# Down's integer weights made one chunk every second round, in a generator of their own

## The chip, the cores and the metric

The kernel runs on one core of a Trainium2 chip. The metric is device time in microseconds; the kernel before was run three times: 442.52, 441.52 and 440.69 us, median 441.52.

## The reference, cut to what matters

```python
x = x + xattn(layernorm(x), ctx, ctx, ...)           # 32 x 64 rows of 512, 8 heads
x = x + ffn(layernorm(x), gate_w, gate_z, gate_s, up_w, up_z, up_s, down_w, down_z, down_s)

def ffn(x, ...):                                     # H = 512, I = 1792, groups of 128
    gate_proj = (gate_w - repeat(gate_z, 128)) * repeat(gate_s, 128)     # 512 x 1792
    up_proj   = (up_w   - repeat(up_z, 128))   * repeat(up_s, 128)       # 512 x 1792
    down_proj = (down_w - repeat(down_z, 128)) * repeat(down_s, 128)     # 1792 x 512
    return (silu(x @ gate_proj) * (x @ up_proj)) @ down_proj
```

The weights are integers of 0 to 15 with a zero point and a scale for every group of 128 rows and each column. All outputs are float32.

## The kernel before, in words

The 32 sequences are taken in pairs (16 pairs of 128 rows), and four pairs make a block of 512 columns, so there are four blocks (t = 0 to 3). The hidden width of 1792 is cut into 14 columns f of 128 (`FC`), the model width of 512 into four groups g (`KT`) and four output parts l (`LC`).

Weights are kept as integers: once, in block 0, the zero point is subtracted from each loaded integer, in place, in the tiles `ng`, `nu` (gate, up) and `nd` (down). The scales are applied later, to the products. Gate and up are subtracted by POOL (L310), in chunks of one group g by 256 or 512 columns, against zeros `z16` that a DMA has spread over the partitions. Down is subtracted by DVE (L301), one chunk of 128 x 512 for each f, against zeros `z8`. `wide` lists the column ranges: 256 columns first (f0, f1), then three times 512 (f2 to f5, f6 to f9, f10 to f13). The tile of `z8` and that of `z16` in the loop have one buffer each: the load of the next range must wait until the last subtraction has read the one before.

After a first stage, whose order is written out by hand (`START`), a loop of rounds runs, 28 rounds (`ROUNDS`) for a block. In a round each of two lanes does one group g of `gate_up` (L627): two pairs of matmuls into `pg` and `pu`, each with a high and a low part of the activations, and ACT multiplies each sum by a quotient of scales before the next group is added (L646). After four groups ACT makes `g` with the silu (L649), DVE makes `h` (L652), and POOL splits it into `hh` and `hl` (L662, L663). Six rounds (`LAG`) behind, `down` (L668) does two output parts l of a column f in a round: a pair of matmuls into `pd` (L681, L684), which DVE adds to `y` (L694). `pd` has two banks, `pg` and `pu` share four. Between these run the steps of attention for the next block (`ROUND_STEPS`), with tiles named for the pairs, as `pv_6to7`, `pe_6to7`, and `q_e_set`, which POOL divides by the softmax sums (L506).

In every round of block 0 the loop calls the generator `weight_steps` (L294), which yields after each subtraction, of gate and up as of down, in one line:

```python
if r < ROUNDS:
    advance(weights, 2 if r < 4 else 1 + r % 2)      # L930, L931
```

The generator goes range by range: eight chunks of gate and up, then down's chunks of that range in a row. Counted out, f0 and f1 come in rounds 4 and 5, f2 in round 5, f3 in 6, f4 and f5 in 7, f6 in 13, f7 in 14, f8 and f9 in 15, f10 in 21, f11 in 22, f12 and f13 in 23. The column f is used by `down` from round 6 + 2f on. The weights of the last two ranges are loaded in rounds 5 and 13 (`load_weights`, L275), issued by POOL; zeros, rows and contexts are loaded by SP, each in its queue's order.

The written order is the input of a scheduler, which sets each engine's final order of instructions; `tc.issue_after` keeps the steps of the inner `with` behind the newest named instructions. [...]

Of the kernel before, what the change touches and what calls it, by code (L numbers as in the profile page):

```python
# [9 lines left out]
F32 = mybir.dt.float32  # L10
# [5 lines left out]
ALU = mybir.AluOpType  # L16
# [10 lines left out]
def kernel(  # L27
# [41 lines left out]
    nc = tc.nc  # L69
    B, D, L = x.shape  # L70
    I = gate_w.shape[1]
    P = 128
    NH, HD = 8, L // 8
    KT = L // P
    FC = I // P
# [38 lines left out]
    with ExitStack() as fast:  # L114
# [53 lines left out]
        wide = [(0, FIRST)] + [(c, CW) for c in range(FIRST, I, CW)]  # L168
# [91 lines left out]
        nd = const.tile([P, FC, L], F32R, tag="nd", name="nd")  # L260
# [6 lines left out]
        def load_wide(w: bass.AP, src: bass.AP, at: int, n: int):  # L267

            newest["POOL"] = nc.gpsimd.dma_start(w[:, :, at : at + n], src[:, :, at : at + n]).ins

        def load_down(at: int, n: int):
            fs = slice(at // P, (at + n) // P)
            newest["POOL"] = nc.gpsimd.dma_start(nd[:, fs, :], down_rows[:, fs, :]).ins

        def load_weights(at: int, n: int):  # L275

            load_wide(ng, gate_rows, at, n)
            load_wide(nu, up_rows, at, n)
            load_down(at, n)

        def load_zeros(at: int, n: int, pool=zeros):

            z16 = pool.tile([P, 2, KT, n], BF16, tag="z16", name=f"z16_{at}")
            for m in range(2):
                nc.sync.dma_start(z16[:, m], z_rows[m, :, at : at + n].partition_broadcast(P))
            return z16

        def load_down_zeros(at: int, n: int):
            z8 = zeros.tile([P, KT, CW], U8, tag="z8", name=f"z8_{at}")[:, : n // P, :]
            zd = z8_dram[at // P * L : (at + n) // P * L]  # L290
            nc.sync.dma_start(z8.rearrange("p f l -> p (f l)"), zd.partition_broadcast(P))
            return z8

        def weight_steps():  # L294

            def of_down(at: int, n: int, z8: bass.AP):
                for i in range(n // P):
                    piece = nd[:, at // P + i, :]  # L300
                    nc.vector.tensor_tensor(piece, piece.bitcast(F32), z8[:, i, :], ALU.subtract)  # L301
                    yield

            late = iter(())
            for at, n in wide:
                z16 = early_zeros.pop(0) if early_zeros else load_zeros(at, n)
                pieces = [(m, g) for g in range(KT) for m in range(2)]
                for m, g in pieces if at else sorted(pieces):
                    piece = (ng, nu)[m][:, g, at : at + n]
                    nc.gpsimd.tensor_tensor(  # L310
                        piece, piece.bitcast(F32), z16[:, m, g, :], ALU.subtract
                    )
                    yield
                yield from late
                late = of_down(at, n, load_down_zeros(at, n))
                if at:
                    yield from late

        def top_steps():

# [377 lines left out]
        def finish(t: int):  # L698

            for a in range(0, PB, SET):  # L700
                p = t * PB + a
                r = rows.tile([P, SET, L], F32, tag="r", name=f"r_{p}")
                nc.sync.dma_start(r, x1_dram[:, p : p + SET, :])
                yield
                py = two_banks(f"py_{p}")
                with in_one_piece() as first_taken:
                    for i in range(SET):
                        for l in range(LC):
                            nc.tensor.transpose(
                                py[:, i, ts(l, P)], y_sb[t, l][:, ts(a + i, P)], ident  # L710
                            )
                            first_taken()
                nc.vector.tensor_tensor(r, py, r, ALU.add)
                nc.sync.dma_start(o_rows[:, p : p + SET, :], r)
                yield
# [23 lines left out]
        def check_bounds():  # L739
            ok = const.tile([P, 3], F32, tag="ok", name="ok")  # L740
            s_abs = const.tile([P, 3 * NS], F32, tag="s_abs", name="s_abs")
            s_2d = s_all.rearrange("p m n -> p (m n)")
            nc.vector.tensor_scalar(s_abs, s_2d, -1.0, None, ALU.mult)
            nc.vector.tensor_tensor(s_abs, s_abs, s_2d, ALU.max)
            s_ok = const.tile([P, 3 * NS], BF16, tag="s_ok", name="s_ok")
            nc.vector.tensor_scalar(s_ok, s_abs, S_MIN, None, ALU.is_ge)
            nc.vector.tensor_scalar(s_abs, s_abs, S_MAX, None, ALU.is_le)
            nc.vector.tensor_tensor(s_ok, s_ok, s_abs, ALU.mult)
            nc.vector.memset(ok, 1.0)
            nc.vector.tensor_reduce(ok[:, 0:1], s_ok, AX.X, ALU.min)  # L750
            top = const.tile([P, 1], F32, tag="top", name="top")
            nc.vector.tensor_reduce(top, n_sum[0], AX.X, ALU.max)
            nc.vector.tensor_scalar(ok[:, 1:2], top, N_MAX**2, None, ALU.is_le)

            z_ok = const.tile([NS, 3, P], BF16, tag="z_ok", name="z_ok")
            nc.vector.tensor_tensor(z_ok[:, 0:2, :], z_nat[:, 0:2, :], z_16, ALU.is_equal)
            nc.vector.tensor_tensor(z_ok[:, 2, :], z_nat[:, 2, :], z_8, ALU.is_equal)
            nc.vector.tensor_reduce(
                ok[:NS, 2:3], z_ok.rearrange("p m n -> p (m n)"), AX.X, ALU.min
            )  # L760
            nc.vector.tensor_reduce(top, ok, AX.X, ALU.min)
            yield
            p_ok = two_banks("p_ok")[0:1, 0, 0:1]
            nc.tensor.matmul(p_ok, top, ones[:, 0:1], start=True, stop=True)
            nc.vector.tensor_scalar(flag, p_ok, float(P), None, ALU.not_equal)


        def advance(steps, n: int = 1):
            for _ in range(n):
                next(steps, None)  # L770
# [26 lines left out]
        with (  # L797
# [9 lines left out]
            for p in range(PB):  # L807
                j, i = divmod(p, SET)
# [7 lines left out]
            def first_banks(name: str):  # L816
                return ps0.tile([P, 2, CW], F32, tag="s", name=name)

            early_zeros, weights = [], weight_steps()

            @contextmanager
# [66 lines left out]
        def two_banks(name: str):  # L888
            return ps_at.tile([P, 2, CW], F32, tag="at", name=name)
# [15 lines left out]
        ROUNDS = 2 * FC  # L905
        LAG = 6
        done = object()
        bounds = check_bounds()
        BOUNDS_AT = 3 * ROUNDS + FC + LC
        LAST_OUT = (NBLK - 1) * ROUNDS + FINISH_AT[1] + 2  # L910
        with ExitStack():
            for r in range(NBLK * ROUNDS + LAG):
                t, k = divmod(r, ROUNDS)
                if k == 0:
                    attend = attention_steps(t + 1) if t + 1 < NBLK else iter(())
                if k == LAG and t > 0:
                    finishing = finish(t - 1)
                next(lanes[0], done)
                advance(attend)
                if r >= LAG:  # L920
                    advance(downs)
                if r >= 2:
                    next(lanes[1], done)

                with ExitStack() as behind:
                    for ins in newest.values():
                        behind.enter_context(tc.issue_after(ins))
                    if r in (5, 13):
                        load_weights(*wide[(5, 13).index(r) + 2])
                    if r < ROUNDS:  # L930
                        advance(weights, 2 if r < 4 else 1 + r % 2)  # L931
                    else:
                        advance(tops, 1 + (r % 4 == 3))
                    if k in FINISH_AT or k + 2 in FINISH_AT or r == LAST_OUT:
                        advance(finishing)
                if r >= LAG:
                    advance(downs)
                if r == ROUNDS:
                    with tc.issue_after(newest["DVE"]):
                        last_quotients()  # L940
                if r == NBLK * ROUNDS:

                    traced = list(nc.cur_bb.bb.instructions)
                    for engine in nc.engines:
                        last = next(i for i in reversed(traced) if i.engine == engine)
                        with tc.issue_after(last):
                            tc.mark_branch_hint_location("other", "LikelyTaken", [engine])
                if r in (BOUNDS_AT, BOUNDS_AT + 4):
                    with tc.issue_after(newest["DVE"]):
                        next(bounds, None)  # L950
# [119 lines left out]
```

## Time and profile before

| what | us |
|---|---|
| time of the profiled execution | 442.62 |
| its span | 440.7 |
| median of the three runs | 441.52 |
| PE busy in the span | 407.3 |
| DVE, ACT, POOL busy in the span | 330.3, 305.9, 280.4 |
| down's 14 subtractions on DVE, first to last start | 52.0 to 129.9 |
| one of them: least, median, most | 0.673, 0.682, 2.385 |
| gate's and up's subtractions of 512 columns on POOL, mean | 1.16 |
| PE busy in 43 to 135 us | 83.8 of 92 |
| PE busy in 150 to 250 us | 99.25 of 100 |

The span is from the first to the last instruction of one profiled execution; some 1.9 us of its time lie outside. Times in the trace count from the span's start. The loop of rounds of block 0 runs from about 40 to 135 us. A matmul of 512 columns starts 0.233 us after the one before it where PE doesn't wait.

### The profile page before, as it was taken

How to read it: one execution, taken by the hardware profiler on the slowest of the kernel's cores; microseconds unless marked ns; L12 is line 12 of the kernel's file. 1: busy time of each engine (PE TensorE's matmuls, PEld its weight loads, DVE VectorE, ACT ScalarE, POOL GpSimd, SP SyncE). 2: the span in 40 equal slices, each digit the busy share in tenths (PEclk: the TensorE clock that was granted, in tenths of full speed). 3: DMA queues.
4: the chain of work that ended last, by engine and by line, in shares of the span. 5: the costliest groups of instructions: out<-in, count | busy, mean ns of one | idle time of the engine just before them, and what ended most of it. 6: DMA issues, size and time to landing. Idle time of an engine off the chain costs nothing.

```text
span 440.7 us, 10359 instructions
## 1 busy us (share of the span) xinstructions
PE 407.3 (92%) x4191; PEld 313.1 (71%) x4191; DVE 330.3 (75%) x514; ACT 305.9 (69%) x469; POOL 280.4 (64%) x292
## 2 busy tenths in 40 slices
PE   4768987989889999999999999989999999999992
PEld 4655755757668776887778787767778888887871
DVE  5988486798779875895879885896869655768673
ACT  2344895555957679776888679656788787777760
POOL 4385858653954447575788668765787878874321
PEclk9999998999999999999999999999999999999998
DMA  6399659188011200311010102400010022200002
GB/s 214 82 276 367 206 150 280 49 243 260 2 49 48 91 9 0 125 70 51 0 50 1 51 6 92 144 1 1 1 50 1 1 60 85 95 1 0 1 4 100
DMA packets 20911, 36.54 MB, mean 83 GB/s; under 512 B 1832, under 2 KB 7416, under 8 KB 20856
## 3 DMA queue, kind: packets, MB, share of 16 engines
q1 hardware_dynamic: 14056, 24.20, 16.7%
q0 software_dynamic: 6192, 11.01, 8.7%
q8 instruction: 35, 0.57, 0.5%
q10 hardware_dynamic: 608, 0.59, 0.4%
q14 instruction: 20, 0.16, 0.1%
HBM read 27.37 MB, written 8.42 MB: 81 GB/s over the span
## 4 chain that ended last, share of the span: by engine, by line
PE 51%; POOL 18%; DVE 11%; issue 11%; ACT 5%; DMA 1%; SPq 0%; POOLq 0%; DVEq 0%; ACTq 0%
PE pu L636 14%; PE pg L636 14%; PE pd L681 7%; PE pd L684 6%; POOL hl L663 5%; POOL squares L333 3%; POOL squares L331 3%; DVE y L694 3%; POOL hh L662 3%; DVE xn_set L112 2%; POOL nu L310 1%; POOL q_e_set L506 1%; ACT pu L646 1%; DVE nd L301 1%; POOL ng L310 1%
## 5 line engine op out<-in xcount | busy, mean ns | idle before, releaser
L694 DVE SCALAR_TENSOR_TENSOR y<-pd,s_all,y 128x512 f32<-128x512 f32 x204 | 150.0, 743 | 43.8 <-PE pd L684 41.1
L646 ACT ACTIVATE pg<-pg,s_q 128x512 f32<-128x512 f32 x168 | 111.6, 666 | 69.0 <-PE pg L636 67.5
L646 ACT ACTIVATE pu<-pu,s_q 128x512 f32<-128x512 f32 x168 | 111.0, 662 | 9.0 <-PE pu L636 9.0
L662 POOL CAST hh<-h 128x512 fp32r<-128x512 f32 x55 | 35.0, 637 | 96.8 <-DVE h L652 95.2
L681 PE MATMUL pd<-hh,nd 128*128 128x512 f32 x224 | 92.7, 414 | 4.0 <-DVE y L694 3.3
L636 PE MATMUL pg<-hTh,ng 128*128 128x512 f32 x224 | 90.4, 403 | 3.1 <-DVE hTl L579 1.6
L636 PE MATMUL pu<-hTh,nu 128*128 128x512 f32 x224 | 91.2, 407 | 1.7 <-POOL nu L310 1.6
L684 PE MATMUL pd<-hl,nd 128*128 128x512 f32 x224 | 89.0, 398 | 0.2 <-DVE hl L660 0.2
L636 PE MATMUL pg<-hTl,ng 128*128 128x512 f32 x224 | 89.1, 398 | 0.0
L636 PE MATMUL pu<-hTl,nu 128*128 128x512 f32 x224 | 89.1, 398 | 0.0
L663 POOL TENSOR_TENSOR hl<-h,hh 128x512 fp32r<-128x512 f32 x55 | 72.1, 1312 | 4.3
L652 DVE SCALAR_TENSOR_TENSOR h<-pu,s_all,g 128x512 f32<-128x512 f32 x56 | 41.8, 746 | 30.2 <-ACT g L649 19.5
L681 PEld LDWEIGHTS pd<-hh,nd 128*128 128x128 f32 x224 | 42.0, 188 | 20.6 <-DVE y L694 7.0
L333 POOL TENSOR_TENSOR squares<-squares 128x512 f32<-128x512 f32 (+1 forms) x46 | 55.1, 1198 | 1.6
L636 PEld LDWEIGHTS pg<-hTh,ng 128*128 128x128 f32 x224 | 42.3, 189 | 17.2 <-ACT pg L646 2.8
L636 PEld LDWEIGHTS pu<-hTh,nu 128*128 128x128 f32 x224 | 42.3, 189 | 16.8 <-POOL nu L310 2.5
L636 PEld LDWEIGHTS pg<-hTl,ng 128*128 128x128 f32 x224 | 42.4, 189 | 9.4
L636 PEld LDWEIGHTS pu<-hTl,nu 128*128 128x128 f32 x224 | 42.4, 189 | 9.0
L649 ACT ACTIVATE g<-pg,s_all 128x512 f32<-128x512 f32 x56 | 38.9, 694 | 14.1 <-PE pg L636 12.5
L684 PEld LDWEIGHTS pd<-hl,nd 128*128 128x128 f32 x224 | 42.1, 188 | 8.4 <-DVE hl L660 0.5
L310 POOL TENSOR_TENSOR nu<-nu,z 128x512 fp32r<-128x512 f32 (+1 forms) x16 | 17.2, 1076 | 4.2 <-DMA nu<-in_L_ffn_up_w_dram 4.2
L310 POOL TENSOR_TENSOR ng<-ng,z 128x512 fp32r<-128x512 f32 (+1 forms) x16 | 17.0, 1069 | 2.1 <-DMA z<-z_dram 2.1
(293 smaller groups left out, 467.9 us busy)
## 6 DMA issues: line engine op xcount, KB each, us to landing
c_set<-in_ctx_dram SPq DMA_DIRECT2D x6, 512.0 KB
x<-in_x_dram SPq DMA_DIRECT2D x6, 512.0 KB
z<-z_dram SPq DMA_DIRECT2D x6, 512.0 KB
ng<-in_L_ffn_gate_w_dram POOLq DMA_DIRECT2D x3, 1024.0 KB, 5.8
nu<-in_L_ffn_up_w_dram POOLq DMA_DIRECT2D x3, 1024.0 KB, 7.7
x_dram<-x SPq DMA_DIRECT2D x6, 512.0 KB
r<-x_dram SPq DMA_DIRECT2D x6, 512.0 KB
out_dram<-r SPq DMA_DIRECT2D x6, 512.0 KB
```

Source lines behind the costliest of these rows:

```text
L310: nc.gpsimd.tensor_tensor(piece, piece.bitcast(F32), z16[:, m, g, :], ALU.subtract)
L331: nc.gpsimd.tensor_tensor(square[:, :n], piece, piece, ALU.mult)
L333: nc.gpsimd.tensor_tensor(total[:, :n], total[:, :n], square[:, :n], ALU.add)
L636: nc.tensor.matmul(acc, w[:, g, ts(f, P)], half[:, g, :], start=(g == 0 and half is hi), stop=(g == KT - 1 and half is lo), skip_group_che ...
L646: nc.scalar.activation(acc, acc, AF.Copy, scale=by)
L649: nc.scalar.activation(g_sb, acc, AF.Silu, scale=by)
L652: ins = nc.vector.scalar_tensor_tensor(h_sb, acc, by, g_sb, ALU.mult, ALU.mult)
L662: nc.gpsimd.tensor_copy(hh, h_sb)
L663: ins = nc.gpsimd.tensor_tensor(hl, h_sb, hh.bitcast(F32), ALU.subtract)
L681: nc.tensor.matmul(pd, w, h_hi[t, f], start=(t, f) != LAST, stop=False, skip_group_check=True)
L684: nc.tensor.matmul(pd, w, h_lo[t, f], start=False, stop=True, skip_group_check=True)
L694: ins = nc.vector.scalar_tensor_tensor(y, pd, by, y, ALU.mult, ALU.add)
```

## The change

Down's subtractions leave `weight_steps` and get a generator `down_steps`, called in rounds of a list `DOWN_AT`: f0 in round 4, f1 in round 5, and every later f in round 2f + 3, three rounds ahead of its use. Each range's `z8` load is issued by the step that makes the range's first chunk. Gate and up keep their rounds, now written as a table, `WEIGHTS_AT`: two in rounds 0 to 3, one or two in rounds 8 to 13 and 16 to 21. Rounds 8 to 13 hold nine calls, of which the ninth (round 13) went to f6 before; now it makes the first chunk of the last range (its `z16` load included), so that all chunks of gate and up in that range are one call earlier.

```diff
         def weight_steps():
-            def of_down(at: int, n: int, z8: bass.AP):
-                for i in range(n // P):
-                    piece = nd[:, at // P + i, :]
-                    nc.vector.tensor_tensor(piece, piece.bitcast(F32), z8[:, i, :], ALU.subtract)
-                    yield
-
-            late = iter(())
             for at, n in wide:
                 z16 = early_zeros.pop(0) if early_zeros else load_zeros(at, n)
                 pieces = [(m, g) for g in range(KT) for m in range(2)]
...
                     yield
-                yield from late
-                late = of_down(at, n, load_down_zeros(at, n))
-                if at:
-                    yield from late
+
+        def down_steps():
+
+            for at, n in wide:
+                z8 = load_down_zeros(at, n)
+                for i in range(n // P):
+                    piece = nd[:, at // P + i, :]
+                    nc.vector.tensor_tensor(piece, piece.bitcast(F32), z8[:, i, :], ALU.subtract)
+                    yield
...
+        WEIGHTS_AT = {r: 2 for r in range(4)}
+        WEIGHTS_AT |= {r: 1 + r % 2 for at in (8, 16) for r in range(at, at + 6)}
+        DOWN_AT = [4, 5] + [2 * f + 3 for f in range(2, FC)]
+        down_weights = down_steps()
...
                         load_weights(*wide[(5, 13).index(r) + 2])
+                    if r in DOWN_AT:
+                        advance(down_weights)
                     if r < ROUNDS:
-                        advance(weights, 2 if r < 4 else 1 + r % 2)
+                        advance(weights, WEIGHTS_AT.get(r, 0))
                     else:
                         advance(tops, 1 + (r % 4 == 3))
```

In the compiled order, on DVE the four chunks f2 to f5 no longer stand together between the y of l = 0 and of l = 1 of column f1: f2 stays there, f3 comes behind `h` of f3, f4 behind the third y of f2, f5 behind the third y of f3, and the later ones likewise, one for each f. On SP the `z8` load of the first range moves behind the context load at 45 us, that of f6 to f9 ahead of the next context load, and that of f10 to f13 behind the `z16` load of the last range. PE's and ACT's order changes by a few places in columns f1 to f10.

## The prediction

> **What bounds the kernel now.** I read the page's slices first (PE at 9 tenths in nearly all from slice 17 on), then tables by stretch, then PE's waits where it is not full.
>
> ```profile
> 135.00:150.00 15.00, 15.00 (x140) 11.65 (x138) 14.20 (x27) 10.93 (x17) 5.73 (x7) 1.00 0.11 36
> 150.00:250.00 100.00, 99.25 (x1047) 76.50 (x1039) 77.06 (x115) 77.31 (x117) 67.48 (x71) 1.00 0.13 44
> ```
>
> Columns: stretch, its length, busy us of PE, PEld, DVE, ACT, POOL, clock, DMA share, GB/s. From 126 us on PE is full, and nothing edited reaches beyond 135 us of before. A microsecond that PE gains in block 0 is therefore kept to the end, unless lost again inside block 0. What PE loses there, as waits between 62 and 130 us (total, times, longest):
>
> ```profile
> PE pd L681 <- DVE y L694: 2.5, 3, 2.0
> PE pu L636 <- POOL nu L310: 1.6, 2, 1.4
> PE pe_6to L515 <- POOL q_e_set L506: 1.1, 1, 1.1
> PE pv_6to L450 <- DVE k_eT_set L427: 1.1, 1, 1.1
> PE pg L636 <- ACT pg L646: 0.3, 1, 0.3
> ```
>
> The first is one place, with the edited instructions in front of it (timeline of DVE; then the stretches, columns as above):
>
> ```profile
> 63.93 0.75 DVE L694 SCALAR_TENSOR_TENSOR y<-pd,s_all,y 128x512 f32<-128x512 f32 x1 [0.34 <-PE pd L684]
> 64.60 4.91 DVE L301 TENSOR_TENSOR nd<-nd,z 128x512 fp32r<-128x512 f32 x4
> 69.51 1.40 DVE L694 SCALAR_TENSOR_TENSOR y<-pd,s_all,y 128x512 f32<-128x512 f32 x2
> ```
>
> ```profile
> 68.33:70.30 1.97, 0.00 (x1) 0.00 (x1) 1.97 (x5) 0.46 (x1) 0.66 (x2) 1.00 1.39 398
> 70.30:71.40 1.10, 1.10 (x5) 0.92 (x6) 1.10 (x2) 0.10 (x1) 1.10 (x2) 0.99 1.36 387
> 71.40:74.80 3.40, 3.40 (x10) 2.64 (x9) 1.01 (x3) 2.48 (x4) 3.32 (x5) 0.50 1.00 284
> ```
>
> I write pd_1_3 for column f = 1, part l = 3, pg_5 for f = 5. Four Down chunks (f2 to f5) stand between the y of l=0 and of l=1 of column f1. Only two pd banks exist, so pd_1_3 waits for y_1_1: PE stands 1.97 us. One microsecond after it resumes, the granted clock is 0.50 for 3.4 us.
>
> **The change part by part.**
>
> *Work.* The same 14 subtractions (0.68 us alone; beside a POOL instruction up to 2.38, the second of the four above), the same four z8 loads, the same 24 gate/up subtractions of the loop. No engine gets more; only order changes, so I compared each engine's compiled instruction order. On DVE, f3, f4, f5 go behind h_3, y_2_2, y_3_2, and so on singly. On POOL the nu0 subtraction of the last 512 columns moves ahead of hh_7, ng2 ahead of hh_8, ng3 ahead of the softmax division (L506). On SP the z8 loads move later.
>
> *A. Start of the loop: 0.* z8 of f0 and f1 (128 KB) is issued behind c_set, which SP issues at 45.13; before it went at 21. f0 waits for the nd weights anyway:
>
> ```profile
> DVE nd L301 <- DMA nd<-in_L_ffn_down_w_dram: 2.3, 1, 2.3
> ```
>
> It starts at 52.01. c_set's packets are through by about 51; 128 KB at 184 to 388 GB/s (the table's rates at 44 to 52 us) is 0.3 to 0.7 us more. Behind f0 on DVE queue mx, less and y_0_0, which has 0.64 us of idle before it; so 0 to 1 us, I take 0.
>
> *B. 64 to 76 us: +3.7.* After y_1_0 comes one chunk (0.98 us in the trace, beside POOL's DMA issues), then y_1_1 at 65.6 and not 69.51; pd_1_3 goes at 67.47 without a wait. Gained: the row step 67.93 to 70.30 less the usual 0.233 us, 2.14. The half clock: nine matmul steps from 71.33 to 74.98 take 3.65 us instead of 9 x 0.233 = 2.10, so 1.55 more. Check by walking: PE reaches pg_5's third matmul pair at 72.2 (it waits for ACT as before) instead of 75.89.
> [...] The row has 0.50 for one window's length, 71.4 to 74.8; in the 3.4 us ahead of it PE was busy 1.45. I take the row: a mostly idle window is enough. The stand of 1.44 us at 124 left the clock at 1.00, so the limit lies between about 1.5 and 2 us.
>
> *C. 76 to 91 us: -0.7.* POOL gains less than PE: its ng0 subtraction must await the ng load (issued 62.87, 5.8 us to land), so it is 1.2 us early, not 3.7. ng3 (behind the layer norm's power, whose input DVE has ready at 82.6) then ends at 84.5, while PE wants it at 83.8 for pg_6's last pair. Before, ng3 ended at 87.57 and PE came at 89.61. Left: 3.0.
>
> *D. 91 to 101 us: +2.0.* The chunks f7 to f9 no longer stand before k_eT: the 1.1 us wait at pv_6to falls to about 0.35 (the key bias follows at once on xn_set), and of the two y waits (0.26, 0.30, with about 0.3 of slow restarts) half remain; pu_7's third pair fits in ahead. By walking, the score matmuls start at 101.0 instead of 105.96 (for equal work). Left: 5.0.
>
> *E. 101 to 120 us.* Here POOL decides.
>
> ```profile
> 107.75 1.17 POOL L310 TENSOR_TENSOR ng<-ng,z 128x512 fp32r<-128x512 f32 x1 [2.13 <-DMA z<-z_dram]
> 118.35 1.90 POOL L506 TENSOR_TENSOR q_e_set<-q_e_set,sm_6to 128x1024 f32<-128x1024 f32 x1
> 120.21 1.68 POOL L310 TENSOR_TENSOR ng<-ng,z 128x512 fp32r<-128x512 f32 x1
> 123.78 1.60 POOL L310 TENSOR_TENSOR nu<-nu,z 128x512 fp32r<-128x512 f32 x1
> ```
>
> ng0 waits for the z16 of the last columns. It was issued at 99.1 behind c_set and the z8 of the last chunks, and none of the three moved a byte while the weights (software queue) ran:
>
> ```profile
> q0 software_dynamic: 1195, 2.38, 135.1%
> ```
>
> That row, of 95 to 101 us, is the only queue of its answer; the weights end near 102, z16 lands 5.7 us later. After: h_5 goes ahead of xn_set, so hl_5 and the weight issues behind it are 4.85 us earlier and the weights end at 97.15; z8 (256 KB, 0.7 us at 379 GB/s) now follows z16. Landing 97.15 + 5.7 - 0.7 = 102.15. From there POOL does, up to the end of the division, seven subtractions at 1.13 (ng0 to ng3; before it were six), hh and hl of f7 and f8 (3.9 together) and the division, 1.90: 102.15 + 7.9 + 3.9 + 1.9 = 115.85. PE's walk brings it to pe_6to at 114.0. It stands 2.1 us there, before 1.12, and starts at about 116.05 instead of 120.31. Left: 4.25.
> [...]
>
> *F. 120 to 126 us: +1.7.* The last nu subtraction ends at 117.7, PE asks at 119.6: the wait of 1.44 (1.7 with restart) goes. Left: 6.0.
>
> *G. Clock after E: -0.8.* A stand of 2.1 us is at the limit found in B; whether it fills most of a window depends on where windows fall. Half of 1.55.
>
> *SP.* z8 of f6 to f9 waits for f5 (about 85.9) and now stands in front of c_set, which waits for pv_6to (93.4) anyway: 0. z8 of f10 to f13 waits for f9 (116.4) with the store of x behind it, wanted by nobody soon: 0; f10 is used at about 121, and z8 of f2 needed under 3 us from 61.11.
>
> *Sum.* 6.0 - 0.8 = 5.2 us. The profiled execution has span 440.7 and time 442.62; 442.62 - 5.2 = 437.4 us. That execution is 1.1 us above the median of the runs, 441.52, perhaps because others missed the slow window; against the median the gain is 4.1 us, 0.9%. About 0.5%, 2.2 us, is what a measurement of this kernel can tell from no change.
>
> **Rivals.**
>
> [...]
>
> 2. *A wait in each round instead of one large one.* Each chunk now stands between two y of one column (f3, f4, f5 ...), and y frees one of two banks. The two cases in the trace cost 0.26 and 0.30 us, 0.3 to 0.4 with restart. If 10 chunks cost 0.35, 3.5 us go: 442.62 - 1.6 = 441.0, no difference to tell. Against it: PE has one or more gate/up pairs (0.47 us each) between most pd pairs.
>
> 3. *Slower: the z16 load is no earlier.* Place: POOL's ng0 of the last columns. If it lands at 107.7 still (c_set or the weights hold it), nu0 delays hh_7 and ng3 the division: q_e ends at 121.4 instead of 120.25. PE is 1.1 us late at pe_6to, gets 0.45 ahead by the vanished nu wait, but has stood over 5 us, so at least one slow window, 1.55: 443.7. It decides from a landing of about 107 on; at 106 it is a tie. For it: POOL is busy from 107.75 to 125 with hardly a gap, so lateness there passes straight to PE. Against: everything that releases the load comes 4 to 5 us earlier.
>
> 4. *f0 late.* If z8 of f0 lands after 53, each microsecond holds pd_0, mx and exp; at 3 us late, 440.5.
>
> **How the numbers follow.** Forecast 0.55 (435.4 to 439.3), rival 1 0.15, rivals 2 and 4 together 0.18, rival 3 0.12. Faster by over 0.5% (under 439.3): 0.70; within: 0.18; slower: 0.12. The range leaves out rival 3 and the far end of rival 1: 434.3 to 441.6.
>
> **What would show it.** No PE stand near 68 us and clock 1.00 up to 100 us (B); a wait of some 0.7 us of PE for POOL's ng, a new one (C); the pv_6to wait under 0.5 (D); ng0's DMA wait ending near 102 and PE's wait for q_e_set about 2 us, the largest left (E); no PE wait for nu after it (F). Wrong, if the slow window appears without a stand before it, if z16 lands after 105, or if pd's waits for y sum to over 2 us.

## The result, and the profile after

The changed kernel takes 443.08 us (median of 12 runs), the kernel before beside it 441.70 us (12 runs): a ratio of 1.0017, 95% interval 0.9999 to 1.0035. So there is no difference that can be told; the forecast was 437.4 us (435.4 to 439.3). The profiled execution took 443.27 us, its span is 441.5.

A stand is time in which PE waits. The stands of PE from 40 to 140 us in the changed kernel that bear on the forecast (us in total, times, longest; lines between them left out):

```profile
PE pe_6to L511 <- POOL q_e_set L502: 2.2, 1, 2.2
PE pd L677 <- DVE y L690: 2.0, 2, 1.4
...
PE pg L632 <- POOL ng L301: 0.9, 1, 0.9
PE pu L632 <- POOL nu L301: 0.7, 1, 0.7
```

The stand at pd_1_3 is down from 2.0 to 0.58 us, and the wait at pv_6to is gone, as forecast; so is the wait of 1.4 for nu near 124. What is new is a stand of 1.4 us at pd_5_1 near 97, behind a subtraction of Down (f6) that waits for its z8:

```profile
96.04 0.69 DVE L312 TENSOR_TENSOR nd<-nd,z 128x512 fp32r<-128x512 f32 x1 [1.16 <-DMA z<-z_dram]
97.45 0.50 PE L677 MATMUL pd<-hh,nd 128*128 128x512 f32 x1 [1.41 <-DVE y L690]
```

And the stand at pe_6to has doubled (the kernel before, then the changed one):

```profile
120.31 1.16 PE L515 MATMUL pe_6to<-w_T,q_e_set 64*64 64x64 f32 x64 [1.12 <-POOL q_e_set L506]
120.56 1.99 PE L511 MATMUL pe_6to<-w_T,q_e_set 64*64 64x64 f32 x64 [2.24 <-POOL q_e_set L502]
```

It costs more than its 2.24 us, as the table by stretch of the changed kernel shows (length, then busy us of PE, PEld, DVE, ACT, POOL; granted clock; DMA share; GB/s):

```profile
91.00:101.00 10.00, 8.45 (x164) 5.88 (x164) 8.12 (x12) 3.79 (x7) 1.86 (x3) 1.00 1.15 329
101.00:119.89 18.89, 16.40 (x126) 11.82 (x124) 15.15 (x21) 15.08 (x22) 14.38 (x13) 1.00 0.28 90
119.89:126.72 6.83, 6.16 (x74) 5.18 (x75) 2.34 (x3) 2.34 (x3) 4.01 (x4) 0.50 0.11 38
```

From 119.89 us, within the stand, the granted clock is 0.50 for 6.83 us. The same products start in the two traces as follows:

| product | before | after | ahead |
|---|---|---|---|
| pe_4to (softmax weights of pairs 4, 5) | 76.56 | 74.22 | 2.34 |
| pv_6to | 96.82 | 94.28 | 2.54 |
| pss_6to (scores) | 105.03 | 104.15 | 0.88 |
| pe_6to | 120.31 | 120.56 | -0.25 |
| po_6to | 126.10 | 127.39 | -1.29 |

(Around pss_6to a few gate and up products change places, so 0.88 is a lower end.) The changed kernel enters the loop 0.5 us late in this trace (its first pg at 39.48 instead of 38.99); 0.4 of it stands already at 15 us (a pq of the first stage, at 15.50 instead of 15.11), before anything edited runs. So what the first bundle of Down gains is 2.8 us. It is gained by 76 us, and all of it is lost between 95 and 127 us.

Why POOL is late for pe_6to stands in its timeline (start, duration, line, operation; in brackets what it waited for), here in the changed kernel; the prediction shows the same work before:

```profile
106.11 1.17 POOL L301 TENSOR_TENSOR ng<-ng,z 128x512 fp32r<-128x512 f32 x1 [4.09 <-DMA z<-z_dram]
107.54 1.17 POOL L301 TENSOR_TENSOR nu<-nu,z 128x512 fp32r<-128x512 f32 x1 [0.26 <-DMA z<-z_dram]
118.61 1.90 POOL L502 TENSOR_TENSOR q_e_set<-q_e_set,sm_6to 128x1024 f32<-128x1024 f32 x1
```

z16 of the last columns lands at 106.11, not at 102.15 as forecast (before: 107.75). The division ends at 120.51, 0.26 later than before. What fills the queues in front of z16, from the list of DMA issues (changed kernel; KB each, us from issue to landing); then SP's issues of z8 and of z16, and the whole traffic of 91 to 95 us:

```profile
ng<-in_L_ffn_gate_w_dram POOLq DMA_DIRECT2D x1, 1024.0 KB, 9.3
nu<-in_L_ffn_up_w_dram POOLq DMA_DIRECT2D x1, 1024.0 KB, 11.7
nd<-in_L_ffn_down_w_dram POOLq DMA_DIRECT2D x1, 1024.0 KB, 15.5
```

```profile
89.10 0.32 SPq L291 DMA_DIRECT2D z<-z_dram  x1
95.92 1.43 SPq L285 DMA_DIRECT2D z<-z_dram  x2
```

```profile
DMA packets 466, 0.93 MB, mean 231 GB/s; under 512 B 14, under 2 KB 14, under 8 KB 466
...
q0 software_dynamic: 333, 0.68, 63.0%
q1 hardware_dynamic: 133, 0.24, 36.4%
```

Before, these three took 5.8, 7.7 and 9.9 us. In the changed kernel SP issues the z8 of f6 to f9 (256 KB) at 89.10, in the middle of POOL's three weight issues (88.47, 89.30, 90.03). From 91 to 95 us the two queues together (q0 the weights, q1 what SP issues) move 231 GB/s, where the next six microseconds have 393. A slow start alone doesn't make this: before, the weights moved 42 GB/s in their first 2.2 us, but 397 from 95 us on. The last weights land near 105.5, and z16, issued at 95.92, comes behind them.

### The profile page after: what moved, and what is told of

Same layout as the page of the kernel before. It is cut to its first block, busy times and chain, and to the rows that moved or that the text cites. A ratio compares the mean times of both kernels' runs of the same rounds, so it can differ in the third digit from the quotient of the medians.

```text
span 441.5 us, 10362 instructions
## 1 busy us (share of the span) xinstructions
PE 409.5 (93%) x4191; PEld 315.7 (72%) x4191; DVE 332.5 (75%) x514; ACT 305.5 (69%) x469; POOL 281.6 (64%) x292
## 4 chain that ended last, share of the span: by engine, by line
PE 52%; POOL 16%; DVE 12%; issue 10%; ACT 5%; DMA 4%; SPq 0%; POOLq 0%; DVEq 0%; ACTq 0%
PE pu L632 14%; PE pg L632 14%; PE pd L677 8%; PE pd L680 7%; POOL hl L659 5%; POOL squares L329 3%; DMA z<-z_dram 3%; POOL squares L327 3%; POOL hh L658 2%; DVE y L690 2%; DVE xn_set L112 2%; POOL q_e_set L502 1%; DVE q_e_set L479 1%; DVE nd L312 1%; DMA x<-in_x_dram 1%
```

## Experiments

All times are medians beside the kernel before on the same chip, and the ratios are to its own medians: 442.23 us (the single edits, both together, f2 to f5 spread), 442.49 (the control, f6 to f13 spread, the group of ng, the filled stand), 442.63 (the last range's Down weights on the runs with early zeros, the tiny instruction) and 441.98 (the same weights as the changed kernel's one edit).

**Two single edits and both together.** POOL's order as before:

```diff
-        WEIGHTS_AT |= {r: 1 + r % 2 for at in (8, 16) for r in range(at, at + 6)}
+        WEIGHTS_AT |= {r: 1 + r % 2 for at in (8, 16) for r in range(at, at + 6)} | {13: 1}
```

> The changed kernel with POOL's order put back: the last range's subtractions begin in round 16 again, so one subtraction fewer (1.15 us) stands before hh of f7 and before the softmax division. Theory (the 256 KB of z8 beside the last weights is the cause): the zeros z16 still land at about 106, PE still stands 1.4 us for f6's chunk near 97; the division ends 1.15 us earlier (119.4), the stand at pe_6to falls from 2.2 to about 1.1, which is below what halves the clock, and a wait for nu of up to 1 us returns: 439.5 to 441.5. Rival (POOL's order alone is the cause): about 438, with the waits at 97 and for z16 harmless. Rival (neither matters, a small wait at each chunk eats the gain): 443, as the changed kernel.

441.08 us, ratio 0.9969 (0.9954 to 0.9984): 0.5% under the changed kernel.

Down's zeros early and small:

```diff
-            z8 = zeros.tile([P, KT, CW], U8, tag="z8", name=f"z8_{at}")[:, : n // P, :]
+            z8 = zeros.tile([P, 2, CW], U8, tag="z8", name=f"z8_{at}", bufs=3)
...
+        ZEROS_AT = {4: [0], 7: [1, 2], 11: [3, 4], 19: [5, 6]}     # round: pairs of columns
...
+                    for j in ZEROS_AT.get(r, []):
+                        z8_of[j] = load_down_zeros(2 * P * j, 2 * P)
```

> The changed kernel with Down's zeros loaded by pairs of columns in three small buffers, f6 to f9 in round 11 (about 77 us) and f10 to f13 behind the last z16, so that no z8 load runs beside the last weights (issued 88.5 to 90.8). Theory: the three weight loads land again 5.8, 7.7 and 9.9 us after issue instead of 9.3, 11.7 and 15.5; f6's chunk does not wait (1.16 us), PE's stand of 1.4 us near 97 goes; z16 lands near 103 instead of 106.1, the division ends near 117.5, PE's stand at pe_6to is under 1 us and the half clock of 6.8 us after it is gone: 437.5 to 439.5. Rival (the z16 load is held by the context load or by the weights, not by z8): z16 at 106, 441.5 to 443. Rival (small waits at each chunk): 442 to 443, waits for y unchanged.

439.57 us, ratio 0.9957 (0.9937 to 0.9977). The traffic of 91 to 95 us, with the weights issued at the same moment as in the changed kernel (88.51 for 88.47):

```profile
DMA packets 727, 1.46 MB, mean 364 GB/s; under 512 B 16, under 2 KB 16, under 8 KB 727
```

Both edits together, called the combined run below:

> Both edits together: Down's zeros early, and POOL's old order. Theory: as with the zeros alone, and the division 1.15 us earlier still, with a wait for nu behind it possible: 437 to 439. If the zeros alone make no difference but POOL's order does: as the run with POOL's order alone. If small waits at each chunk eat the gain: 442 to 443.

439.04 us, ratio 0.9930 (0.9905 to 0.9956). The traffic of 91 to 95 us in this run, and then its z16, its division and its pe_6to:

```profile
DMA packets 792, 1.60 MB, mean 401 GB/s; under 512 B 16, under 2 KB 16, under 8 KB 791
```

```profile
103.55 1.16 POOL L301 TENSOR_TENSOR ng<-ng,z 128x512 fp32r<-128x512 f32 x1 [3.32 <-DMA z<-z_dram]
114.60 1.90 POOL L500 TENSOR_TENSOR q_e_set<-q_e_set,sm_6to 128x1024 f32<-128x1024 f32 x1
```

```profile
116.55 1.16 PE L509 MATMUL pe_6to<-w_T,q_e_set 64*64 64x64 f32 x64 [0.97 <-POOL q_e_set L500]
```

With the 256 KB of z8 out of the way, 1.46 MB (zeros alone) and 1.60 MB (both, where the weights leave 0.55 us earlier) move in the four microseconds instead of 0.93; in the combined run the weights take 6.4, 9.1 and 11.9 us. The wait of f6's chunk for its z8 (1.16 us) and PE's stand behind it at pd_5_1 are gone in both runs with early zeros, and z16 comes 1.8 us (zeros alone) and 2.6 us (both) earlier. POOL's order is worth something of its own: with it put back, PE's stand at pe_6to is 1.1 us instead of 2.2, with the zeros where the change put them. The two gains are 0.5% and 0.6% apart and 0.9% together, each against the changed kernel; with some 0.2% of noise on each, whether they fully add can't be told. The early zeros missed their forecast in two points: z16 landed at 104.31 and not near 103, and the stand at pe_6to stayed at 2.24 us, since PE came earlier too; but no half clock followed it (see the last section).

**What the spreading itself is worth.** On the combined run: all of Down's chunks in bundles again (control), only f2 to f5 spread, only f6 to f13 spread.

```diff
-        DOWN_AT = [4, 5] + [2 * f + 3 for f in range(2, FC)]
+        DOWN_AT = [4, 5, 5, 6, 7, 7, 13, 14, 15, 15, 21, 22, 23, 23]        # control
+        DOWN_AT = [4, 5, 7, 9, 11, 13, 13, 14, 15, 15, 21, 22, 23, 23]      # f2 to f5 spread
+        DOWN_AT = [4, 5, 5, 6, 7, 7] + [2 * f + 3 for f in range(6, FC)]    # f6 to f13 spread
```

In the first and the third the zeros of f2 to f5 are loaded in round 5 and not 7.

> Control: the same early loads of Down's zeros by pairs and POOL's old order as in the combined run, but all of Down's chunks in their bundles, as in the kernel before. Theory: the zeros cost the kernel before nothing (its z8 never ran beside the weights), so this is the kernel before within 0.3%: 441 to 442.5, with the stand near 68 and the wait at pv_6to back. Rival (the gain of the combined run comes from the early zeros and not from spreading the chunks): 439 to 440.

> The last kernel, with f6 to f13 in their bundles again (rounds 13, 14, 15, 15 and 21, 22, 23, 23): only f2 to f5 are spread. Theory: the stand of 1.97 us near 68 and its half clock are gone (2.8 us, of which POOL's ng takes 0.7 at once), the wait of 1.1 us at pv_6to and the y waits near 97 stay: 439 to 440.5. Rival (what is gained at 68 is lost again wholly by 120, since POOL's division decides): 441.5, as the kernel before.

> The combined run with f2 to f5 in their bundle again (rounds 5, 6, 7, 7) and only f6 to f13 spread. Theory: PE stands about 2 us again near 68, with a half clock behind it in many executions, and z16 and the division come 2 to 3 us later; what the other columns gain (1.1 at pv_6to, 0.5 at y) stays in part: 440 to 441.5. If the two parts add, its gain over the control and the first bundle's gain over the control sum to the combined run's gain (3.2 us over the kernel before). If only the later columns matter: 439, as the combined run.

| chunks spread | us | ratio to before | against the control |
|---|---|---|---|
| none (control) | 444.49 | 1.0052 (1.0034 to 1.0070) | |
| f2 to f5 | 440.80 | 0.9970 (0.9953 to 0.9987) | -3.7 us |
| f6 to f13 | 443.25 | 1.0021 (1.0008 to 1.0033) | -1.2 us |
| all | 439.04 | 0.9930 (0.9905 to 0.9956) | -5.5 us |

The control missed its forecast: it is 0.5% slower than the kernel before. On DVE the layer norm's statistics (1.27 us) stand behind the bundle in its compiled order, ahead of it before, and PE's longest wait for y is 2.3 us instead of 2.0:

```profile
PE pd L675 <- DVE y L688: 2.9, 3, 2.3
```

The run with f6 to f13 spread has the same order and the same 2.3 us, and missed its forecast (440 to 441.5) too; f2 to f5 came 0.3 us over theirs. So with the chunks in bundles the early zeros showed no gain, and the control measures differences between its own variants, not from the kernel before. Those nearly add up: 3.7 and 1.2 apart, 5.5 together. The order on PE is the same work with other places for a few products, so this is the value of spreading where no z8 meets the weights, the longer stand of the bundle included.

**The group of ng that PE waits for at pg_6, two rounds earlier.**

```diff
-            ... | {13: 1}
+            ... | {11: 3, 12: 1, 13: 0}
```

> The combined run with the last two subtractions of the third range two rounds earlier, so that on POOL the one for ng's fourth group stands ahead of the power of a layer norm for which POOL waits 2.4 us, and the z16 buffer comes free earlier (z16 goes out beside the x load of 87 us, ahead of the last weights). Theory (POOL's chain decides 80 to 120 us): PE's wait for ng at pg_6 (1.1) goes, POOL's wait for z16 (3.3) falls under 1, so the division ends 3 us earlier and the waits for q_e_set (1.0) and nu (0.9) go: 436 to 437.5. Rival (z16, x and the weights together crowd the queues, as z8 did): the weights land late instead, ng's first chunk waits for the weights, 439 to 441.

439.29 us, ratio 0.9931 (0.9906 to 0.9955), no gain over the combined run. The rival came true:

```profile
99.18 1.17 POOL L301 TENSOR_TENSOR ng<-ng,z 128x512 fp32r<-128x512 f32 x1 [4.54 <-DMA ng<-in_L_ffn_gate_w_dram]
```

The z16 buffer is free earlier, its 1 MB goes out just ahead of the weights, and ng's weights land 11.2 us after issue instead of 6.4. POOL is done with the division at 114.76, 1.7 us earlier than in the combined run, but PE then waits 1.8 us for the last nu, whose subtraction stands behind hh and hl of f9.

**The last range's Down weights later.** They are wanted only at about 117 us; here POOL issues them behind hl of f6.

```diff
                     if r in (5, 13):
-                        load_weights(*wide[(5, 13).index(r) + 2])
+                        at, n = wide[(5, 13).index(r) + 2]
+                        load_wide(ng, gate_rows, at, n)
+                        load_wide(nu, up_rows, at, n)
+                        if r == 5:
+                            load_down(at, n)
+                    if r == 16:
+                        load_down(*wide[3])
```

On the combined run:

> The combined run (early zeros, POOL's old order) with the last range's Down weights (1 MB, wanted only at about 117) issued behind hl of f6, some 10 us later, so that 1 MB less stands ahead of z16. Theory (z16 comes when the bytes ahead of it are through, at about 390 GB/s): z16 lands some 2.5 us earlier, near 101, when POOL is free; its wait of 3.3 us falls under 1; the division ends near 114; PE's wait for q_e_set (1.0) goes, and the wait for nu (0.9) stays or grows, since its subtraction stands behind hh and hl of f9, which wait for PE: 437.5 to 439. Rival (z16 is bound by the moment of its issue behind the context load): z16 as before at 103.5, 439.

438.89 us, ratio 0.9926 (0.9901 to 0.9950). z16 lands at 99.16, in part because SP now issues it at 90.60 and not behind the context load at 95, which the expectation had not seen. The rest went as its theory said: the wait for q_e_set is gone, that for nu grew to 1.8.

On the run with early zeros, with POOL's order as the change has it:

> The changed kernel with early zeros and the Down weights of the last range issued behind hl of f6, POOL's order as changed. Here z16 stands ahead of the context load in SP's order. Theory: z16 lands by 98 and no longer holds POOL; the changed order, which puts the last nu subtraction directly behind the division, then has no waits behind it: division ends near 115.5, waits of PE for q_e_set and nu under 0.5 each, the half clock at 120 gone: 436 to 438. Rival (queues crowd, as when z16 stood beside all three weights): ng lands at 97 or later, POOL waits for it, 439 to 440.

436.53 us, ratio 0.9867 (0.9841 to 0.9893): the best kernel found, and faster than both (its five runs all lie below the lowest of either). z16 came later than its theory had it (100.00, not 98), and the waits behind it went as said. Its POOL, PE at pe_6to, and its table by stretch:

```profile
100.00 1.17 POOL L301 TENSOR_TENSOR ng<-ng,z 128x512 fp32r<-128x512 f32 x1 [1.38 <-DMA z<-z_dram]
113.07 1.90 POOL L500 TENSOR_TENSOR q_e_set<-q_e_set,sm_6to 128x1024 f32<-128x1024 f32 x1
114.93 1.16 POOL L301 TENSOR_TENSOR nu<-nu,z 128x512 fp32r<-128x512 f32 x1
```

```profile
115.67 1.16 PE L509 MATMUL pe_6to<-w_T,q_e_set 64*64 64x64 f32 x64
```

```profile
101.00:120.00 19.00, 18.75 (x210) 14.16 (x212) 16.03 (x22) 15.91 (x24) 16.75 (x15) 1.00 0.22 65
120.00:135.00 15.00, 15.00 (x129) 12.34 (x122) 14.03 (x25) 11.05 (x18) 5.49 (x6) 1.00 0.19 71
```

The order that costs 2 us where z16 is late (first experiment) is here the better one by 2.4 us: the last nu subtraction follows the division at once, and no wait of PE for POOL is left behind pg_6.

On the changed kernel itself, as its one edit:

> The changed kernel with one edit alone: the Down weights of the last range (1 MB) issued behind hl of f6, some 8 us later; z8 stays where the change put it, beside the gate and up weights at 89 us. The z16 load now stands ahead of the context load. Theory (what decides is how many bytes are ahead of z16, not z8's 256 KB by themselves): z16 lands by 101, POOL hardly waits, the division ends near 115.5, PE stands under 1 us at pe_6to, no half clock at 120; f6's chunk still waits up to 1 us: 437.5 to 439. Rival (z8's many small packets are what slows both queues, so it must go out elsewhere): weights and z16 late still, 440.5 to 442.

438.56 us, ratio 0.9923 (0.9899 to 0.9948). Its z16 and division, and its traffic of 91 to 95 us:

```profile
101.71 1.16 POOL L301 TENSOR_TENSOR ng<-ng,z 128x512 fp32r<-128x512 f32 x1 [1.54 <-DMA z<-z_dram]
114.62 1.91 POOL L502 TENSOR_TENSOR q_e_set<-q_e_set,sm_6to 128x1024 f32<-128x1024 f32 x1
```

```profile
DMA packets 493, 0.98 MB, mean 245 GB/s; under 512 B 15, under 2 KB 15, under 8 KB 493
```

The slow traffic beside z8 is still there, f6 still waits 1.09 us, and PE stands behind it as before:

```profile
97.43 0.51 PE L632 MATMUL pu<-hTh,nu 128*128 128x512 f32 x1 [1.75 <-DVE h L648]
```

And yet the gain appears: 1% under the changed kernel. So f6's own wait costs little by itself, z8 beside the weights is one way to be late, and what counts here is when z16 lands. This edit also lets z16 out at 91.3 instead of 95.9, since SP now has it ahead of the context load; how much of the gain is the 1 MB and how much the earlier issue was not separated.

**The stand at pe_6to filled.** Five idle products, whose results are overwritten, in front of the true ones (ten records in the trace), on the changed kernel, all else in its order:

```diff
                 with self.in_order() as first_taken:
+                    for _ in range(5 if self.p == 6 else 0):
+                        nc.tensor.matmul(
+                            self.pe[: self.n * NH, 0].rearrange("p n d -> p (n d)")[:, : 2 * P],
+                            self.sm, self.x[:, 0, : 2 * P], start=True, stop=True,
+                        )
```

> The changed kernel with five idle products (256 columns, float32, some 0.36 us each, written to pe_6to's own bank before the true ones) in PE's stand ahead of pe_6to; all else in the same order. Theory: the clock is granted by windows of 3.41 us on a fixed grid, and one follows at half speed when PE was busy for less than about 1.9 us in the one before; the fill takes that away behind the stand. The stand itself stays (POOL decides), the half clock of 6.8 us in the changed kernel's trace is gone, the mean clock of the runs rises from 0.986 to about 0.990: 440.5 to 442. Rival (the half clock has another cause): no change of clock, 443 or, with the fill late, 443.5.

441.35 us, ratio 0.9981 (0.9968 to 0.9994): 0.4% under the changed kernel, with five products more. PE at pe_6to, the fill and then the true products:

```profile
118.95 2.33 PE L511 MATMUL pe_6to<-x,sm_6to 128*16 128x256 f32 x10
121.71 1.16 PE L516 MATMUL pe_6to<-w_T,q_e_set 64*64 64x64 f32 x64 [0.43 <-POOL q_e_set L502]
```

pe_6to is no earlier (z16 landed at 106.82 here), but the products after it run at a granted clock of 1.00 (119.73 to 126.55 us; 0.50 in the changed kernel from 119.89). The mean granted clock of its runs is 0.992 (median of 22), of the changed kernel's 0.986 (12), of the kernel before 0.991 (57). One window of 3.41 us at half clock lowers the mean over 440 us by 0.5 x 3.41 / 440 = 0.0039; by an estimate from these medians, which are rounded to 0.001, the changed kernel thus has about 1.3 such windows more than the kernel before, 1.7 us each of lost work: some 2.2 us, half of what the combined run wins back.

**The tiny instruction beside the division.** rs_6to (128 x 2) took 1.86 us in the changed kernel, 0.15 before; in DVE's timeline it stands between the one chunk that is left and y_1_1:

```profile
65.11 1.11 DVE L312 TENSOR_TENSOR nd<-nd,z 128x512 fp32r<-128x512 f32 x1
66.14 1.86 DVE L388 TENSOR_SCALAR rs_6to<-mv_6to 128x2 f32<-128x2 f32 x1
67.92 1.40 DVE L690 SCALAR_TENSOR_TENSOR y<-pd,s_all,y 128x512 f32<-128x512 f32 x2
```

```diff
-            0.scores 0.highest | 0.less 0.exp | 0.sums 0.divide | | 1.stats 1.scale |
-            0.turn 0.turn_out | ...
+            0.scores 0.highest | 0.less 0.exp | 0.sums 0.divide | | |
+            0.turn 0.turn_out 1.stats 1.scale | ...
```

> The combined run with the layer norm statistics of pairs 6 and 7 two rounds later, so that the tiny rs_6to instruction (128 x 2) no longer runs beside POOL's softmax division, where it took 1.64 to 1.87 us instead of 0.15. Theory (a DVE instruction beside POOL's division is held until that ends, and y_1_1 behind it): y_1_1 comes 1.5 us earlier, PE's wait at pd_1_3 (0.4 here) goes; worth 0.4 to 1 us: 438 to 438.7. Rival (the next DVE instruction beside the division is held instead): no change, 439.

438.71 us, ratio 0.9916 (0.9891 to 0.9941): not to be told from the combined run (0.9930). The hold is gone, rs_6to takes 0.16 us:

```profile
69.83 0.16 DVE L386 TENSOR_SCALAR rs_6to<-mv_6to 128x2 f32<-128x2 f32 x1
```

y_1_1 starts at 66.52, and PE no longer waits for y near 68; but that wait was only 0.2 us in the combined run, where the hold of rs_6to was 1.64, so there was no more to win. The hold explains a part of B in the changed kernel (PE stood 0.58 us at pd_1_3), and none of the combined run's remaining time that could be told.

## Why the prediction was wrong, step by step

*Where it failed: SP, "z8 of f6 to f9 waits for f5 ... and now stands in front of c_set, which waits for pv_6to (93.4) anyway: 0".* The load was costed by its place in SP's queue alone. It was freed by f5 just when POOL issued the last weights, which the same change had moved earlier, and it ran beside them. What it did: f6's own wait (1.16 us, and PE's 1.4 at pd_5_1), some 0.5 MB of transfers lost in four microseconds (0.93 against the 1.46 MB with early zeros alone), and z16 behind them. The early zeros alone win back 0.6%, some 2.7 us. Of these, f6's wait is the small part: in the run with the Down weights later PE's stand behind it is 1.75 us, and the time is 1% better all the same. Between the forecast (4.1 us gained on the median) and the result (1.4 us lost) lie 5.5 us; beside these 2.7, 0.9 are B's below, and the rest is not told apart. The load and the weights were each placed in time in the prediction (f5 "about 85.9", the weights "4.85 us earlier" than 91.37), and never laid side by side.

*E, "the weights end at 97.15 ... Landing 97.15 + 5.7 - 0.7 = 102.15".* Both halves were off. POOL's weight issues came 2.9 us earlier, not 4.85, and the transfers took 9.3 to 15.5 us instead of 5.8 to 9.9. z16 landed at 106.11. From there to the end of the division POOL took 14.4 us, where 13.7 were forecast (a wait of 0.26 for nu's zeros and a subtraction of 1.64 are in it). So the division ended at 120.51, where 115.85 was forecast; 4.0 of these 4.7 us are z16's. Without the collision, in the combined run, z16 lands at 103.55: even there the last weights need 2 us longer than before, now with the x load of 87 us directly ahead of them; whether that load is the reason was not tried.

*A, "0".* It held: f0 waits 2.35 us, now for its z8, and starts at 52.55 instead of 52.01, which is the lateness of the whole loop.

*B, "+3.7".* The stand and its half clock went, as said; 2.8 us came. The term that was too large is y_1_1 "at 65.6": the prediction let one chunk stand before it and overlooked rs_6to, which stands between them in DVE's order and held y_1_1 to 67.92. That f2 to f5 bring 3.7 us against the control is luck: it is a difference in the whole time, from a control that has a longer stand than the kernel before.

*C, "-0.7".* PE's new wait for POOL's ng is there, 0.9. *D, "+2.0".* The wait at pv_6to went as forecast (PE is 2.54 us ahead there), and 1.1 us of the lead was lost again 3 us later at f6's z8 (pq_6to starts at 99.05 instead of 100.47). Rival 2, a wait at every chunk, did not appear: of the waits for y that the change made, 0.58 us are rs_6to's and 1.41 those of one late load.

*F, "+1.7".* The wait of 1.4 for nu near 124 went, as said; another, at 117.6, grew from 0.15 to 0.66 us.

*G, "-0.8", half a chance of one slow window.* The stand of 2.2 us was followed by two windows in this trace. Between pe_6to and po_6to PE falls back by 1.04 us although F gave back its wait of 1.4 (1.6 with the restart), so they cost 2.6. The mean clock says about 1.3 windows more than before.

*Rival 3* named the place (POOL's ng0 of the last columns), the mechanism and nearly the price: "at 106 it is a tie", 443.7 from 107 on; it landed at 106.11, for 443.08. What spoke "against" it, that all that releases the load comes 4 to 5 us earlier, was true in part of the issue (95.92 for 99.09, 3.2 us) and not of the bytes in front of it.

*The queues and the clock.* On the queues the prediction took the row of 95 to 101 us, in which z8 and c_set moved nothing, to mean that z16 comes wholly behind the weights. The runs don't show that: 333 packets of weights and 133 from SP's queue, where z8 stood, share 91 to 95 us above. The row could not decide it: SP issued c_set at 97.97, only 3 us before the row's end, and in the changed kernel too an SP load issued at 95.43 has hardly moved (0.01 MB) by 98, and SP's queue moves 0.32 MB beside the weights from 98 to 101. From 91 to 95 us both queues together moved 231 GB/s, 364 with the zeros early. On the clock the prediction took the trace, PE busy for 1.45 us of 3.4 being enough for half clock, and the runs agree (1.44 and 1.19 us in the last section). Its limit by the length of a stand ("between about 1.5 and 2 us") does not hold: with POOL's order as before, half clock followed a stand of 1.13 us with two small waits ahead of it, and the stands of 2.24 (early zeros) and 1.75 us (Down weights later) went without.

*Rival 1's chance of 0.15 and the 434.3 us of its far end*, a gain beyond the forecast. No run shows the terms for it: z16 landed at 106.11 in the changed kernel, and the fastest of its 12 runs took 440.38 us.

## To carry to other kernels

When an edit moves a load, lay its flight beside every other flight of those microseconds, with the bytes on all queues ahead of the one that someone waits for; a place in one queue says nothing of that. Where several loads leave together, send the one wanted last behind the others: taking 1 MB of late-wanted weights out of the way, and the earlier issue of z16 that came with it, was worth 1% on the changed kernel. An order that looks worse while its input is late can be the better one once it is not, so judge orders again after the wait in front of them is gone.

## What the runs showed of the hardware that was not expected

*The granted clock changes on a grid of 3.41 us that lies elsewhere from trace to trace.* In the kernel before, the changed kernel and the run with early zeros (three tables by stretch, cut at the grid):

```profile
67.98:71.39 3.41, 1.44 (x7) 0.91 (x6) 3.41 (x6) 0.76 (x2) 2.10 (x3) 1.00 1.37 396
71.39:74.81 3.42, 3.42 (x10) 2.66 (x9) 1.03 (x3) 2.50 (x4) 3.34 (x5) 0.50 0.99 283
```

```profile
116.47:119.89 3.42, 1.19 (x4) 0.32 (x3) 2.22 (x3) 2.97 (x4) 3.42 (x3) 1.00 0.03 7
119.89:123.30 3.41, 2.74 (x66) 2.53 (x67) 1.16 (x1) 0.69 (x1) 3.33 (x4) 0.50 0.18 64
123.30:126.72 3.42, 3.42 (x9) 2.65 (x9) 1.18 (x2) 1.65 (x3) 0.68 (x1) 0.50 0.04 13
```

```profile
113.91:117.32 3.41, 2.52 (x10) 1.42 (x8) 1.31 (x3) 3.38 (x6) 3.41 (x4) 1.00 0.03 5
117.32:120.73 3.41, 1.98 (x68) 1.78 (x69) 2.04 (x3) 1.67 (x3) 3.41 (x3) 1.00 0.01 2
120.73:124.15 3.42, 3.42 (x75) 2.67 (x74) 2.23 (x4) 2.19 (x4) 1.46 (x3) 1.00 0.02 5
```

A stand of 2.2 us that falls into one window leaves PE 1.19 us busy, and half clock follows; the same stand across a boundary leaves 2.52 and 1.98, and nothing follows. In ten of the traces, cut so from about 10 to 400 us, every window shows 1.00 or 0.50 and nothing between. Of the windows at 1.00 none with PE busy for 1.92 us or more was followed by half clock, every one under 1.7 was, and between 1.71 and 1.91 both occur; of those at 0.50 one was, the second window of the changed kernel above, with PE busy for 2.74. Ahead of that stretch, from 0.42 to 7.25 us, the changed kernel has two windows with PE busy for 0.00 and 1.15 us, and the clock stays at 1.00. An eleventh has an exception, in the run with the Down weights later on the changed kernel, so the busy time as the trace has it is not quite what decides:

```profile
95.01:98.42 3.41, 1.66 (x20) 1.00 (x9) 2.01 (x3) 1.33 (x2) 0.90 (x2) 1.00 1.20 372
98.42:101.83 3.41, 3.41 (x74) 2.64 (x74) 2.06 (x3) 1.69 (x3) 1.87 (x3) 1.00 1.12 378
```

So half clock followed windows in which PE was busy for up to 1.91 of 3.41 us, and what a stand costs is in part a matter of chance: the changed kernel's 12 runs go from 440.38 us, at a mean clock of 0.994, to 444.89, at 0.982; the best kernel's five, with no stand of that size, from 436.12 to 436.77.

*A load of 256 KB can take more than its bytes.* Beside z8 (one row of zeros spread to 128 partitions) the queues moved 231 and 245 GB/s in the two traces shown, without it 364 and 401. With nothing beside it, from 122.1 to 123.7 us of the changed kernel, a z8 of the same size moves at some 160 GB/s (all of it in this answer for 122 to 124 us):

```profile
DMA packets 144, 0.26 MB, mean 131 GB/s; under 512 B 16, under 2 KB 16, under 8 KB 144
```

That it is spread is not the reason by itself: z16, spread as well, moved 322 GB/s from 104 to 107 us of the kernel before. By the queues' counts of 91 to 95 us its packets are little smaller than those of the weights: 133 for 0.24 MB beside 333 for 0.68. Why the weights are slower beside them was not tried.

*A DVE instruction of two columns can take 1.86 us* when POOL's division has started before it: the division ran from 65.81 to 67.97, rs_6to from 66.14 to 68.00. Moved away, it takes 0.16. The runs show the time, not what holds it.
